# Gate tiles issued by SyncE between the row moves, and a new hand-written order of all steps

## The chip, the core and the metric

The kernel runs on one NeuronCore of a Trainium2 chip. The metric is the device time of one execution in microseconds (us), the median of several runs. Engines are named as in the profile: PE is TensorE (PEld its weight loads), DVE is VectorE, ACT is ScalarE, POOL is GpSimd, and SP is SyncE, which here only issues DMAs.

## What is computed

The reference is one conditional block on x of 32 x 128 tokens by 512 features, read as 8 x 1024 x 512 with 32 conditions of 512 (all in float32):

```python
m = mask[:, :, None]
shift, scale, gate_msa = jnp.split(jax.nn.silu(t) @ ada_w + ada_b, 3, axis=1)
norm = jnp.where(m, _layernorm(x) * (1.0 + scale[:, None]) + shift[:, None], 0.0)
fwd = gelu(norm @ ssm_w1 + ssm_b1) @ ssm_w2 + ssm_b2
bwd = flip(gelu(flip(norm) @ bwd_w1 + bwd_b1) @ bwd_w2 + bwd_b2)
x = x + gate_msa[:, None] * jnp.where(m, fwd + bwd, 0.0)
shift_mlp, scale_mlp, gate_mlp = jnp.split(jax.nn.silu(t) @ ffada_w + ffada_b, 3, axis=1)
ff_norm = _layernorm(x) * (1.0 + scale_mlp[:, None]) + shift_mlp[:, None]
return x + gate_mlp[:, None] * (gelu(ff_norm @ ff_w1 + ff_b1) @ ff_w2 + ff_b2)
```

Masked tokens are few. The first half (the part under the mask) is done for those tokens alone in the opening, some 82 us. The second half, the feed-forward with 512 -> 1024 -> 512 features for all 4096 tokens, is the rest, and only the rest is touched by the change.

## The kernel before, in words

**Tiling.** The 32 batches of 128 tokens are worked in four pairs (p = 0 to 3) of two sides; a side is four batches (G = 4, 512 tokens). Both products of the feed-forward are done by Strassen's scheme in the variant of Winograd, with seven block products instead of eight: the first product has seven streams (1, 2, 5, 6, 3, 7, 4) of seven products each (`6P5` is product P5 of stream 6; L1155), the second product has P1, P5, P2, P6 for two column blocks U and V (`P1U0`; L1387) and three inner products, P3, P7 and P4, that are cut into seven again (`6i3` is part 6 of P3; L1473). What is saved in matmuls is paid in additions on DVE, POOL and ACT.

**What stands around the matmuls.** In the first product, `j` steps (L1207, DVE) add a finished PSUM bank to earlier results and so free the bank; `g` steps (L1125, ACT) apply the gelu. For the second product, `sa0`, `se0`, `sa1`, `se1` (L1283, ACT) seed the PSUM accumulators a_o and e_o with the bias; a_o takes the bank that stream 3 leaves, so `sa0` waits for `3j21`. `k51` and `ke1` (L1303 and L1307, ACT) keep and re-seed the second column block, before `P2V`. `C1i3`, `C5i3` and so on (L1500, ACT) copy inner products out of PSUM. `F00` (L1294, DVE) adds two blocks of the hidden layer.

**The next pair.** While pair p is multiplied, pair p+1 is made ready: `b` steps (L937, DVE) take statistics, POOL forms the root (L945), `n0i` (L955, a DVE TENSOR_SCALAR) and `n1i` (L959, ACT) normalise batch i of side 0 and side 1 into xn, `z` steps (L1808, DVE) transpose 32x32 blocks in place. Then 32 small DMAs `m` (L991, 64 KB each, 16 for a side, issued by SP) move the turned rows from xn to xT, and 32 `c` steps (L968, ACT) scale and shift xT in place. All four `z` of a side come before its first `m`, and all 16 `m` of a side before its first `c`. At the end of the pair, `nW1` and `nW2` (L1109, SP) load weight sums and `n1P1`, `n1P5` and so on are the first products of the next pair.

**The gate.** The output of the feed-forward is multiplied by the gate (L1349 on POOL for side 0, L1331 on DVE for side 1). A gate tile is 128 x 4 x 512 float32, 1 MB, read from gate_rows in DRAM and spread to all partitions (`gate_tile`, L912 to L919). `lg0` and `lg1` load that of side 0 and of side 1. It lies in the same SBUF buffer as weight sums of the first product: gate 0 comes after `7P4` has read its buffer, gate 1 after the last product of stream 4.

**What sets the order.** From about 82 us on all five engines are scheduled by hand: every step is put under its name, and `steps.run(ORDER.get(p, "").split())` issues the steps of pair p in the order of a table of names, one table for each pair. Each engine works off its own instructions in that order, and waits by semaphores for the others. The table also fixes what stands behind what on SP.

Of the kernel before, what the change touches and what calls it, by code (L numbers as in the profile page):

```python
# [22 lines left out]
def kernel(  # L23
# [49 lines left out]
    nc = tc.nc  # L73
# [839 lines left out]
    def gate_tile(p, side):  # L913
        t = gp.tile([P, G, D], F32, tag=f"g{side}", name=f"gate_{p}_{side}", bufs=1)
        nc.gpsimd.dma_start(
            t,
            gate_rows[ts(2 * p + side, G), :].unsqueeze(0).to_broadcast([P, G, D]),
        )
        return t  # L919
# [345 lines left out]
    class SecondProduct:  # L1265
# [9 lines left out]
        def load_gate(self, side):  # L1275
            self.gate[side] = gate_tile(self.p, side)
# [362 lines left out]
    def windows(put, q, f, first, last):  # L1639
# [50 lines left out]
        for w in range(first, last):  # L1690
# [6 lines left out]
            6P5 5P3 6P1 load1 6c5 5k12 6s 3P5 5P7 b00 6P2 x17 6w12 b01 6P6 5j22 6k11 6w22 load0 3P1  # L1697
            6a11 5P4 b02 3c5 6e 5k21 6P3 6P7 3w22 b03 3s b10 6k12 b11 3P6 W3 w30 3P2 7P5 6j22 b12
            7c5 3w12 7P1 6P4 v0 w20 6a12 7s r0 6j21 W4 3k11 4P5 7P2 7w12 3e 6a22 n00 7P6 b13 3P7
            7w22 3P3 4P1 7k11 v1 7e L11 3j22 7P7 n03 n02 4c5 3k12 3P4 r1 4s 7j22 se0 l1 6a21 7P3 4P6  # L1700
            g1222 3j21 sa0 z00 L22 4P2 n01 7P4 7k12 n12 z01 z02 n13 L12 4k11 g2222 z13 4w12 n10 P1U0
            4w22 7j21 F00 P1U1 4e z03 se1 sa1 L21 m003 g2211 4P7 z12 z10 m032 g1221 w70 m013 4j22
            P1V0 P1V1 g2122 w71 m002 w21 4P4 m012 n11 lg0 F02 4P3 g22L P5U0 z11 m001 P5U1 w72 m023
            4j21 F12 m103 m022 T0 g2121 lg1 m133 F10 m100 4k12 w22 m021 m121 k50 m120 w23 m131 ke0
            P5V0 P5V1 m000 m110 k51 ke1 P2U0 m132 g2212 w31 m123 P2U1 m011 m113 m111 m010 B0 P2V1
            m112 P2V0 K000 T1 P6U1 B1 w40 m130 m102 m122 m101 P6U0 c103 w32 c130 w41 c122 U0 c101
            G000 c111 U1 K001 R000 E0 S1i3 c131 w42 m033 m030 c110 5i3 m020 S2i3 1i3 P6V0 c123 m031
            S1i7 C5i3 C1i3 S3i7 5i7 c100 c020 6i3 C5i7 G001 w43 c003 c032 V6i3 S2i7 J30 1i7 P6V1
            S3i3 c012 S4i3 c120 C1i7 c132 w33 c121 w73 c113 6i7 c011 c000 c133 7i3 c002 3i3 c102
            V6i7 E1 C7i3 c010 7i7 2i3 S4i7 c112 V7i3 K010 C7i7 J70 J31 S1i4 R001 3i7 2i7 V7i7 c030  # L1710
            5i4 c001 S2i4 A1 c022 1i4 c013 c031 4i3 J71 C1i4 4i7 E20 c021 6i4 G110 S3i4 A2 n1P5 K011
            G010 C5i4 E21 n1c5 G011 V6i4 n1P1 S4i4 nW1 n1s R010 c033 7i4 J40 c023 2i4 R110 G111 R111
# [9 lines left out]
            3k11 3e 7P6 b11 7w12 6j21 W4 7P2 v0 3P7 6a22 3P3 b12 7k11 4P5 3j22 4P1 3P4 3k12 x27 7e
            4c5 F00 4s 6a21 3j21 7P7 7w22 b13 7j22 se0 sa0 L11 g2211 7P3 4P6 4P2 v1 g1222 7P4 r0 r1
            P1U0 n01 n00 lg0 g1221 4k11 n03 7k12 L12 4w12 F02 l1 n02 P5U0 z01 n12 z00 n13 z03 n11
            z02 n10 L22 m023 4e m012 P5U1 z10 4w22 7j21 z13 z11 sa1 m001 m033 k50 P1U1 m013 L21 4P7
            z12 se1 m032 4P3 m022 m011 g22L P1V0 ke0 4j22 m002 4P4 m000 g2122 m030 P2U0 T0 4j21 m111
            m103 lg1 g2121 F10 m110 g2222 m003 4k12 P1V1 F12 B0 g2212 P5V1 m121 m031 P5V0 m122 T1
            m021 m112 k51 m120 m101 P2U1 B1 ke1 m020 m100 m010 P2V1 K000 m133 P2V0 K001 m131 U0 m113
            c012 P6V1 G000 m130 m132 c022 c020 U1 c002 c003 m102 P6V0 R000 S1i3 c011 c023 E1 5i3
            S2i3 c000 1i3 C5i3 S1i7 S3i3 c001 m123 c111 P6U1 c112 c123 c122 5i7 c120 c133 c110 P6U0  # L1730
            C5i7 c021 C1i3 1i7 c013 6i3 c010 E0 S2i7 V6i3 C1i7 c132 S4i3 n1P1 c102 c130 S3i7 6i7 J30
            c101 c100 c103 G001 S4i7 V6i7 7i3 c113 c121 2i3 3i3 C7i3 c131 c033 V7i3 K010 S1i4 J70
            5i4 S2i4 2i7 J31 C5i4 A1 c030 7i7 1i4 3i7 C7i7 G010 A2 n1P5 V7i7 C1i4 J71 6i4 A3 S3i4
            S4i4 E20 R010 4i3 V6i4 G110 c032 K011 n1c5 4i7 J40 n1s R110 7i4 E21 2i4 c031 3i4 V7i4
            n1P2 n1P6 G111 o00 n2P5 C7i4 n1k11 J41 G100 R100 A4 n1e n2c5 nt11 n2P1 4i4 G011 R011
            n1P3 n1k12 n2s nt12 G101 nt10 R101 nW1 n1P7 R001 n2P2 n1j22 n2P6 o10 n5P5 o01 n2k11 X0
            n5P1 n5c5 n1P4 nt13 nW2 R111 o11 n2w12 n2e nt20 nt22 n2P7 n5s n2w22 nt23 nx30 nt21 nx31
# [12 lines left out]
            4k12 k51 ke1 P2V1 P2V0 m132 m033 P6U1 K000 lg1 c023 m101 c000 m123 P6U0 m112 c010 m131  # L1750
# [367 lines left out]
```

## Time and profile before

| what | us |
|---|---|
| three runs: median (lowest to highest) | 459.79 (458.73 to 461.62) |
| the profiled execution: time | 461.43 |
| its span, first to last instruction | 459.7 |
| PE busy in the span | 440.8 (96%) |
| DVE / POOL / ACT busy | 337.8 / 266.4 / 205.0 |

The span is what the views show, in us from its start; 1.73 us of the profiled execution's time lie outside. Matmuls are pipelined and their ends are modelled, so that neighbouring rows overlap by some 0.15 us: what a matmul group takes is read from the distance of starts. A row of the timeline gives start, duration, engine, line, operation, the tiles written and read, the shapes, the number of instructions, and in brackets the idle time of the engine before it with what ended that.

### The profile page before, as it was taken

The page shows a single profiled execution, that of the slowest core. Times are in us where ns is not written, and L with a number is a line of the kernel's source. Part 1 is how long each engine was busy: PE and PEld are TensorE (multiplying, and loading weights), DVE is VectorE, ACT ScalarE, POOL GpSimd, SP SyncE. Part 2 cuts the span into 40 slices and gives each one's busy share as a digit, 9 for nine tenths or more (in the row PEclk, how much of TensorE's full clock was granted, in tenths as well). Part 3 has the DMA queues.
Part 4 walks back from the last instruction along what each step waited for, and adds up shares of the span by engine and source line. Part 5 has one row for each costly group of instructions (what it writes and reads, how often), then busy time and mean ns, then how long its engine had stood idle before and what let it go on. Part 6 is the DMA issues. An engine that isn't in the chain of part 4 may idle for free.

```text
span 459.7 us, 7036 instructions
## 1 busy us (share of the span) xinstructions
PE 440.8 (96%) x2435; PEld 374.2 (81%) x2435; DVE 337.8 (73%) x592; ACT 205.0 (45%) x453; POOL 266.4 (58%) x234
## 2 busy tenths in 40 slices
PE   8999999999999999999999999979969999999992
PEld 4884674788888998887889988868869988888992
DVE  5798798789996689889742998995516995444265
ACT  3133126353662963536648435257473344471120
POOL 4211550279923993897449858973395426832891
PEclk9999999999999999999999999999979999999998
DMA  7999449993088108741670197309820273112014
GB/s 256 374 395 398 158 89 323 305 336 119 7 220 122 27 17 315 258 121 80 138 141 13 48 312 234 114 3 186 147 34 1 74 269 109 52 70 115 0 47 140
DMA packets 57044, 70.89 MB, mean 154 GB/s; under 512 B 34740, under 2 KB 36108, under 8 KB 55982
## 3 DMA queue, kind: packets, MB, share of 16 engines
q1 hardware_dynamic: 50590, 59.33, 42.3%
q0 software_dynamic: 4160, 10.54, 7.5%
q10 hardware_dynamic: 2256, 0.54, 0.7%
q8 instruction: 21, 0.34, 0.3%
q14 instruction: 17, 0.14, 0.1%
HBM read 56.71 MB, written 13.70 MB: 153 GB/s over the span
## 4 chain that ended last, share of the span: by engine, by line
PE 70%; DMA 6%; POOL 6%; DVE 6%; issue 5%; SPq 3%; ACT 2%; POOLq 0%; ACTq 0%; DVEq 0%
PE a_m L1155 14%; PE e_m L1155 11%; PE e_o L1387 9%; PE a_o L1387 9%; PE one_P L1473 6%; PE po_s L222 6%; SPq L991 3%; PE a_o L1473 3%; DMA xT<-xn 3%; PE e_o L1473 2%; PE five_P L1473 2%; PE ph_s L681 2%; PE ph_s L205 2%; DMA x<-in_x_dram 1%; ACT xT L968 1%
## 5 line engine op out<-in xcount | busy, mean ns | idle before, releaser
L968 ACT ACTIVATE xT<-xT,modT 128x128 f32<-128x128 f32 x112 | 46.1, 485 | 14.0 <-DMA xT<-xn 13.8
L1182 POOL TENSOR_TENSOR ha<-p_m,ha 128x512 f32<-128x512 f32 x20 | 25.8, 1292 | 45.5 <-ACT ha L1197 36.4
L1349 POOL TENSOR_TENSOR t<-t,gate 128x512 f32<-128x512 f32 x16 | 24.4, 1524 | 44.3 <-ACT t L1343 44.3
L1207 DVE TENSOR_TENSOR hb<-a_m,hb 128x512 f32<-128x512 f32 x40 | 27.2, 679 | 13.4 <-PE a_m L1155 13.3
L1125 ACT ACTIVATE hb<-hb,biasT 128x256 f32<-128x256 f32 x64 | 28.4, 500 | 16.2 <-DVE hb L1207 15.9
L1197 ACT COPY ha<-e_m 128x512 f32<-128x512 f32 x32 | 18.6, 584 | 37.2 <-PE e_m L1155 37.2
L904 POOL DMA_INDIRECT x<-x_rows,slot_i x24 | 30.1, 1255 | 7.7 <-issue 6.2
L1505 DVE TENSOR_TENSOR xn_d<-one_P,xn_d 128x256 f32<-128x256 f32 x24 | 10.1, 422 | 30.7 <-PE one_P L1473 24.4
L1387 PE MATMUL a_o<-fw,ha 128*128 128x256 f32 x128 | 29.7, 380 | 3.0 <-ACT a_o L1283 3.0
L1387 PE MATMUL a_o<-t,s 128*128 128x256 f32 x128 | 31.3, 395 | 0.0
L1387 PEld LDWEIGHTS a_o<-fw,ha 128*128 128x128 f32 x128 | 24.2, 190 | 6.7 <-ACT a_o L1283 3.4
L1387 PE MATMUL e_o<-fw,s 128*128 128x256 f32 x128 | 29.1, 379 | 0.0
L1387 PE MATMUL e_o<-fw,ha 128*128 128x256 f32 x128 | 28.6, 379 | 0.0
L222 PE MATMUL po_s<-w,h_s 128*128 128x512 f32 x64 | 28.4, 594 | 0.0
L1182 POOL TENSOR_TENSOR hb<-p_m,hb 128x512 f32<-128x512 f32 x20 | 26.1, 1307 | 2.6 <-DVE hb L1207 2.0
L1387 PEld LDWEIGHTS a_o<-t,s 128*128 128x128 f32 x128 | 24.8, 199 | 3.3
L1387 PEld LDWEIGHTS e_o<-fw,s 128*128 128x128 f32 x128 | 24.3, 190 | 3.3
L1387 PEld LDWEIGHTS e_o<-fw,ha 128*128 128x128 f32 x128 | 24.3, 190 | 3.3
L1125 ACT ACTIVATE ha<-e_m,biasT 128x256 f32<-128x256 f32 x48 | 19.9, 467 | 13.7 <-PE e_m L1155 12.6
L1155 PE MATMUL a_m<-xT,tw 128*128 128x256 f32 x96 | 24.8, 382 | 0.3 <-DVE e_m L1188 0.3
L1169 ACT COPY p_m<-e_m 128x512 f32<-128x512 f32 x27 | 15.8, 585 | 18.9 <-PE e_m L1155 18.8
L1155 PE MATMUL e_m<-s,fw 128*128 128x256 f32 x92 | 23.7, 380 | 0.0
(281 smaller groups left out, 1160.5 us busy)
## 6 DMA issues: line engine op xcount, KB each, us to landing
x<-in_x_dram SPq DMA_DIRECT2D x16, 512.0 KB, 6.4
tw<-t_rows SPq DMA_DIRECT2D x16, 512.0 KB, 4.2
gate<-gate_rows POOLq DMA_DIRECT2D x8, 1024.0 KB, 6.5
out_dram<-x SPq DMA_DIRECT2D x15, 512.0 KB, 4.0
xT<-xn SPq DMA_DIRECT2D x104, 64.0 KB, 2.2
tw<-t_rows SPq DMA_DIRECT2D x16, 384.0 KB
ada_f<-in_L_cond_ffada_w_dram SPq DMA_DIRECT2D x4, 768.0 KB, 14.7
ada_a<-in_L_cond_ada_w_dram SPq DMA_DIRECT2D x4, 512.0 KB, 3.5
```

The lines of the kernel that those rows point to most:

```text
L222: nc.tensor.matmul(po, h[f][:, ts(i, P)], w[:, f, :], start=(f == 0 and seeded is None), stop=(f == HC - 1), skip_group_check=seeded is no ...
L904: nc.gpsimd.indirect_dma_start(out=xs[i // G][i % G // 2][:, i % 2], out_offset=None, in_=x1_rows, in_offset=bass.IndirectOffsetOnAxis(ap= ...
L968: nc.scalar.activation(out, src, AF.Identity, bias=shift, scale=scale)
L1125: nc.scalar.activation(dst[:, n], src[:, n], AF.Gelu_apprx_tanh, bias=biasT[:, f : f + 1])
L1155: nc.tensor.matmul(bank[:, ts(n, QT)].rearrange("p (i b c) -> p i b c", i=2, c=R), self.w_block(j, product)[:, ts(n, P)], self.x_block(j, ...
L1169: nc.scalar.copy(self.p5[j], self.fives[j].rearrange("p (n s) -> p n s", n=2))
L1182: nc.gpsimd.tensor_tensor(self.place(RESULT[j], c), self.p5[j], other, ALU.add)
L1197: nc.scalar.copy(self.place(RESULT[j], c), src)
L1207: nc.vector.tensor_tensor(dst, a, other, ALU.add)
L1349: nc.gpsimd.tensor_tensor(view, view, self.gate[side][:, 2 * c : 2 * c + 2, part], ALU.mult)
L1387: nc.tensor.matmul(bank[:, ts(i, D // 2)], src[:, k, ts(i, P)], w[:, k, :], start=False, stop=True, skip_group_check=True,)
L1473: nc.tensor.matmul(out[:, i % out.shape[1]], src[:, k, ts(i, P)], w[:, k, :], start=(start and (i == 0 or out.shape[1] == 1) and k == 0), ...
```

## The change

Two things are changed. `gate_tile` issues its DMA from SP's queue instead of POOL's:

```diff
     def gate_tile(p, side):
         t = gp.tile([P, G, D], F32, tag=f"g{side}", name=f"gate_{p}_{side}", bufs=1)
-        nc.gpsimd.dma_start(
+        nc.sync.dma_start(
             t,
             gate_rows[ts(2 * p + side, G), :].unsqueeze(0).to_broadcast([P, G, D]),
         )
```

And the tables of all four pairs hold the same names in another order. The number of steps, and of instructions on every engine but SP and POOL, stays the same. One row of each table, pair 2:

```diff
-            6P4 b10 n02 W4 3P6 6j21 7P2 z02 7k11 3e 6a22 7w12 n00 x36 7P6 7e 4P5 4P1 3P7 4c5 7w22
+            r0 6P4 7P2 3e b10 7P6 3w22 6j21 7k11 n00 W4 7e 6a22 4P5 n03 z03 4P1 3P7 L11 4c5 7w22
...
```

What that does to the engines is shown at three places, all in pair 2. In the names, a number behind a tile's name is a buffer's; xT_0 and xn_0 are side 0, xT_1 and xn_1 side 1 of the next pair.

First SP, from the last weight sums of pair 2's first product to the first of the next pair's. Before:

```order
L1109 DMA tw_1_2279<-t_rows 128x768
L991 DMA xT_0_2518<-xn_0_2432 32x8x64 x14
L991 DMA xT_1_2614<-xn_1_2552 32x8x64
L991 DMA xT_0_2518<-xn_0_2432 32x8x64
L991 DMA xT_1_2614<-xn_1_2552 32x8x64 x3
...
L991 DMA xT_1_2614<-xn_1_2552 32x8x64 x12
L1109 DMA tw_0_2899<-t_rows 128x1024
```

Now:

```order
L1109 DMA tw_1_2297<-t_rows 128x768
L991 DMA xT_0_2520<-xn_0_2442 32x8x64 x9
L915 DMA gate_0_2586<-gate_rows 128x2048
L991 DMA xT_0_2520<-xn_0_2442 32x8x64 x7
L991 DMA xT_1_2614<-xn_1_2565 32x8x64 x16
L915 DMA gate_1_2842<-gate_rows 128x2048
L1109 DMA tw_0_2895<-t_rows 128x1024
```

The gate of side 0 stands behind nine moves, that of side 1 behind all 32, and all moves of side 0 come before the first of side 1. In pair 0 the first gate stands ahead of all moves, in pair 1 behind seven; the second stands behind all 32 in both. In pair 3, which has no moves, both stand behind each other, side 1 first, as they did on POOL.

Then DVE in pair 2, where the last batches of side 0 are normalised while stream 3 ends (a_m_3, its bank, is freed by the second L1207 on it). Before:

```order
L1175 TENSOR_TENSOR e_m_4_2453<-a_m_4_2454,ha_2221 128x512
L955 TENSOR_SCALAR xn_0_2432<-x_2270,mv_0_2344,rstd_0_2345 128x4x4x32
L1207 TENSOR_TENSOR hb_2222<-a_m_3_2365,hb_2222 128x2x256
L1808 STREAM_TRANSPOSE xn_0_2432<-xn_0_2432 128x4x4x32
L1207 TENSOR_TENSOR hb_2222<-a_m_7_2402,hb_2222 128x2x256
L955 TENSOR_SCALAR xn_0_2432<-x_2268,mv_0_2344,rstd_0_2345 128x4x4x32
...
L937 BN_STATS st_1_2_2489<-x_2328 128x6
```

Here the row left out is the second L1207 on a_m_3 (`3j21`), right behind the fourth L955. Now:

```order
L1808 STREAM_TRANSPOSE xn_0_2442<-xn_0_2442 128x4x4x32 x2
L1207 TENSOR_TENSOR hb_2230<-a_m_3_2357,hb_2230 128x2x256
L1175 TENSOR_TENSOR e_m_4_2448<-a_m_4_2449,ha_2229 128x512
L1207 TENSOR_TENSOR hb_2230<-a_m_7_2411,hb_2230 128x2x256
L955 TENSOR_SCALAR xn_0_2442<-x_2289,mv_0_2344,rstd_0_2345 128x4x4x32
L1808 STREAM_TRANSPOSE xn_0_2442<-xn_0_2442 128x4x4x32
...
L937 BN_STATS st_1_1_2490<-x_2322 128x6
L938 BN_AGGR mv_1_2347<-st_1_1_2490 128x2
L955 TENSOR_SCALAR xn_0_2442<-x_2291,mv_0_2344,rstd_0_2345 128x4x4x32
```

Again `3j21` is the row left out; it now stands behind three of the four L955, and the fourth follows it.

Last ACT in pair 2, where the scaling of xT meets the copies of the second product. Before:

```order
L1343 COPY t_100_2674<-e_o_1_2554 128x512
L968 ACTIVATE xT_0_2518<-xT_0_2518,modT 128x4x32 x5
L968 ACTIVATE xT_1_2614<-xT_1_2614,modT 128x4x32
L968 ACTIVATE xT_0_2518<-xT_0_2518,modT 128x4x32
L968 ACTIVATE xT_1_2614<-xT_1_2614,modT 128x4x32 x2
L968 ACTIVATE xT_0_2518<-xT_0_2518,modT 128x4x32 x2
L1500 COPY xn_d_2705<-one_P_2697 128x2x128
...
L1500 COPY xn_d_2705<-five_P_2692 128x2x128
```

Now:

```order
L1307 COPY e_o_0_2484<-a_o_0_2485 128x512
L968 ACTIVATE xT_0_2520<-xT_0_2520,modT 128x4x32 x2
L1303 COPY p_o_1_2632<-e_o_1_2532 128x512
L1307 COPY e_o_1_2532<-a_o_1_2533 128x512
L968 ACTIVATE xT_0_2520<-xT_0_2520,modT 128x4x32 x4
L1343 COPY t_000_2647<-e_o_0_2484 128x512
...
L1343 COPY t_100_2668<-e_o_1_2532 128x512
L968 ACTIVATE xT_0_2520<-xT_0_2520,modT 128x4x32
L1500 COPY xn_d_2703<-one_P_2690 128x2x128
L968 ACTIVATE xT_1_2614<-xT_1_2614,modT 128x4x32
...
L1500 COPY xn_d_2703<-five_P_2680 128x2x128
```

The first copy of an inner product (L1500 from one_P, `C1i3`) stood behind three scalings of side 1; now it stands ahead of them all, and the second (from five_P, `C5i3`) behind two. On the other hand two scalings of side 0 now stand ahead of `k51` and `ke1` (L1303 and L1307 on e_o_1).

More of the change, by code (lines that the diff above doesn't have):

```diff
@@ L1696 @@
         0: """
[L1697 to L1712, printed above, removed]
@@ new lines @@
+            sa1 m002 w70 z10 P5U1 m033 4P4 g2122 g22L m021 w22 4j21 P1V1 m012 z11 4P3 m022 g2121 k50
+            F12 P1V0 F10 m020 P5V1 w31 m011 m133 m030 B0 P5V0 w32 ke0 k51 w23 P2U1 P2U0 m023 T1 4k12
+            m010 m032 ke1 K000 T0 P2V0 m111 m102 B1 m100 m031 P2V1 P6V1 w40 m113 K001 w71 m112 G000
+            U0 m000 m130 m101 U1 m110 w72 R000 m001 m003 S1i3 P6V0 w41 c030 m132 S2i3 c033 5i3 c001
+            C5i3 m120 c032 1i3 c022 m122 m121 C1i3 w42 m131 P6U1 c003 6i3 c013 S1i7 m103 c023 V6i3
@@ L1722 @@
[L1722 to L1737, printed above, removed]
@@ new lines @@
+            7k12 g2211 z02 b13 g1221 4P2 F02 v1 n00 L12 z00 m033 r1 l1 g2212 4w12 m031 4k11 m013 L22
+            m032 7P4 n10 P1U1 P1U0 P5U1 7j21 n12 sa1 P5U0 n11 4e n13 se1 z12 m012 m000 m020 lg0 k50
+            g2222 4P7 L21 4P3 P1V0 m030 z13 4w22 m001 4j22 g2122 z10 ke0 4P4 T0 m010 m003 m002 4j21
+            P1V1 m011 z11 m103 P2U1 g2121 F10 m023 g22L m130 m022 m132 F12 m131 m100 m021 T1 m101 B0
+            m122 P5V0 P5V1 4k12 k51 P2U0 ke1 K000 B1 P2V0 U0 c000 G000 m102 P2V1 R000 U1 c012 m111
@@ L1770 @@
[L1770 to L1774 removed]
+            6P1 6P5 5P3 5P7 5j22 6c5 3P1 3P5 5P4 6s W3 6P2 5k12 6P6 5k21 6k11 6w12 6e 7P5 6a11 3c5
```

100 lines of the change are left out of this document (61 added, 39 removed).

## The prediction

> **What bounds the kernel now.** I read the busy shares first, then PE stretch by stretch, then what ended PE's idle times, then the rows around them.
>
> ```profile
> PE 440.8 (96%) x2435; PEld 374.2 (81%) x2435; DVE 337.8 (73%) x592; ACT 205.0 (45%) x453; POOL 266.4 (58%) x234
> ```
>
> PE is the bound on average. The windows show how evenly; they are pairs 0 to 3 and what follows the last matmul (length, then PE's busy time and records, ending with the granted clock and DMA).
>
> ```profile
> 98.20:188.46 90.26, 89.58 (x494) 79.93 (x493) 78.03 (x123) 48.09 (x108) 62.87 (x48) 1.00 0.50 139
> 188.46:278.94 90.48, 89.49 (x494) 80.05 (x493) 70.13 (x113) 48.61 (x108) 65.70 (x51) 1.00 0.48 135
> 278.94:377.77 98.83, 92.27 (x493) 82.20 (x492) 72.16 (x108) 48.71 (x110) 58.94 (x49) 0.97 0.44 110
> 377.77:451.11 73.34, 73.34 (x421) 66.63 (x419) 36.15 (x54) 26.19 (x58) 46.33 (x38) 1.00 0.20 69
> ```
>
> Pairs 0, 1 and 2 hold the same matmuls, and pair 2 takes 8.4 us more. How far each lies over its matmuls alone follows from undisturbed rows of the chain of waits:
>
> ```profile
> 103.96 2.59 PE a_m L1155 x12
> 415.06 10.36 PE e_o L1387 x48
> 349.00 0.89 PE one_P L1473 x8
> ```
>
> A product of the first kind (x4) takes 0.863, a unit of the second (x8) 1.727, an inner part (x8) 0.89. A pair has 49, 16 and 21 of them: 42.3 + 27.6 + 18.7 = 88.7 us. So pair 0 loses 1.6, pair 1 1.8, pair 2 10.1. PE's waits from 98 us on name most of it:
>
> ```profile
> PE one_P L1473 <- ACT xn_d L1500: 3.6, 1, 3.6
> PE a_o L1387 <- ACT a_o L1283: 3.0, 1, 3.0
> PE a_m L1155 <- DVE e_m L1175: 1.0, 1, 1.0
> ```
>
> The two long ones are in pair 2:
>
> ```profile
> 306.61 3.72 PE L1387 MATMUL a_o<-fw,ha 128*128 128x256 f32 x16 [3.00 <-ACT a_o L1283]
> 340.70 2.05 PE L1473 MATMUL one_P<-inner_more,si_P 128*128 128x128 f32 x8 [3.56 <-ACT xn_d L1500]
> 342.54 3.62 PE L1387 MATMUL a_o<-t,s 128*128 128x256 f32 x8
> 345.96 1.25 PE L1473 MATMUL one_P<-inner_more,ha 128*128 128x128 f32 x8
> 347.05 1.06 PE L1473 MATMUL five_P<-t,si_P 128*128 128x128 f32 x8
> ```
>
> Behind the second wait PE runs at half speed: from start to start the three groups take 1.84, 3.42 and 1.09 us where 0.89, 1.73 and 0.89 are usual, 2.84 us lost (the 0.97 above is this). So pair 2 lost 3.0 + 3.56 + 2.84 = 9.4 by these two waits, and 0.7 otherwise.
>
> **The first wait, the seed.** DVE, ACT and POOL around 303 us:
>
> ```profile
> 300.90 4.43 DVE L955 TENSOR_SCALAR xn<-x,mv,rstd 128x512 f32<-128x512 f32 x1
> 305.25 0.68 DVE L1207 TENSOR_TENSOR hb<-a_m,hb 128x512 f32<-128x512 f32 x1
> ```
>
> ```profile
> 305.96 0.59 ACT L1283 COPY a_o<-fb 128x512 f32<-128x512 f32 x1 [4.15 <-DVE hb L1207]
> ```
>
> ```profile
> 302.56 1.26 POOL L1220 TENSOR_TENSOR hb<-hb 128x512 f32<-128x512 f32 x1
> 303.79 1.25 POOL L1220 TENSOR_TENSOR ha<-ha 128x512 f32<-128x512 f32 x1
> 305.12 1.34 POOL L1182 TENSOR_TENSOR ha<-p_m,ha 128x512 f32<-128x512 f32 x1
> ```
>
> ```profile
> L955 DVE TENSOR_SCALAR xn<-x,mv,rstd x12: 507/586/4431, 113.8 to 300.9; 128x512 f32<-128x512 f32 x12
> ```
>
> ```profile
> 98.20:188.46 90.26, 3.17 (x4) 1.00 0.50 139
> 188.46:278.94 90.48, 2.00 (x4) 1.00 0.48 135
> 278.94:377.77 98.83, 7.60 (x4) 0.97 0.44 110
> ```
>
> One normalisation takes 4.43 us where the median is 0.59 (the last three rows are the busy time of the four L955 of each pair). It ends at 305.33, just behind the first gap in POOL's row of additions (305.04 to 305.12). `3j21`, behind it on DVE, is late by 3.8, and so is the seed.
>
> **The second wait, the moves.** The 32 moves on SP in pairs 0, 1 and 2; then for pair 2 SP's waits for its own DMAs, and the landing times (min/median/max) of moves and of gates:
>
> ```profile
> 127.38 23.64 SPq L991 DMA_DIRECT2D xT<-xn  x32
> ```
>
> ```profile
> 218.79 22.72 SPq L991 DMA_DIRECT2D xT<-xn  x32
> ```
>
> ```profile
> 309.04 27.01 SPq L991 DMA_DIRECT2D xT<-xn  x32
> ```
>
> ```profile
> SPq L991 <- DMA xT<-xn: 5.1, 4, 2.9
> ```
>
> ```profile
> DMA to landing us min/median/max: 2.2/2.3/9.9
> ```
>
> ```profile
> DMA to landing us min/median/max: 8.0/9.0/10.1
> ```
>
> In pair 2 the moves take 27.0, of which SP waits 5.1 for moves that land late, while two gates of 1 MB are under way beside them. Without these waits a move takes 21.9 / 32 = 0.68 to issue, and lands 2.2 later. The first move is itself late, since its transposes stand behind the slow L955 on DVE. At the end of this the copy sits behind scalings of side 1 on ACT:
>
> ```profile
> 337.89 2.42 ACT L968 ACTIVATE xT<-xT,modT 128x128 f32<-128x128 f32 x6 [3.18 <-DMA xT<-xn]
> 340.21 0.35 ACT L1500 COPY xn_d<-one_P 128x256 f32<-128x256 f32 x1
> ```
>
> **The change part by part.** *Gates off POOL.* Eight issues of 0.6 us leave POOL, and its wait in front of one:
>
> ```profile
> 318.40 0.55 POOL L915 DMA_DIRECT2D gate<-gate_rows  x1 [4.53 <-PE a_m L1155]
> 327.44 1.69 POOL L1349 TENSOR_TENSOR t<-t,gate 128x512 f32<-128x512 f32 x1 [8.48 <-ACT t L1343]
> ```
>
> The next POOL step idles 8.5 us for ACT anyway: worth 0. If that cover were gone it would be worth at most 0.6 a gate.
>
> *Gates onto SP.* Each costs SP about one issue, 0.7. That delays the moves behind `lg0` and, behind `lg1`, only `nW1`. What a gate does to moves behind it in one queue the trace does not show. The bounds: nothing, since even alone on POOL's queue it lands in 4.9 (pair 3's first, below) and SP could issue seven moves in that time; and the 5.1 us of pair 2, where two gates disturb. I take 1.5, nearer the lower end, since one gate is left in the way and the other waits until all moves are issued. The gates' users are far enough: gate 1 now leaves behind the last move, at about 330 in pair 2, lands by 340 even at the worst 10.1 us, and is first read by DVE at 358.3 (the first row; the second is all pairs together). In pair 0 it leaves some 24 us behind the first move, at 152, and has landed by 162, against 167.4.
>
> ```profile
> L1331 DVE TENSOR_TENSOR e_o<-e_o,gate x2: 693/696/699, 358.3 to 368.2; 128x512 f32<-128x512 f32 x2
> ```
>
> ```profile
> L1331 DVE TENSOR_TENSOR e_o<-e_o,gate x8: 683/692/700, 167.4 to 449.2; 128x512 f32<-128x512 f32 x8
> ```
>
> ```profile
> DMA to landing us min/median/max: 4.9/6.0/7.1
> ```
>
> By the Trainium skill, page "DMA: Bandwidth & Descriptors", section "Issuing engines are not separate DMA queues", all issuers share the same 16 engines, so another queue alone changes only who spends the issue time; the late landings above, with the gates on another queue, agree. By that rule alone the sum would be 0, which is the first rival; it says nothing against `lg1` leaving after the moves.
>
> *The seed.* In pair 2 `3j21` now has three L955 ahead of it instead of four, one statistic less and one transpose more: 0.6 + 0.85 - 0.62, some 0.8 us of plain work less. Its product 3P4 still stands three products ahead of P1 on PE. The seed is due at 303.4 (306.6 less the wait and the overlap of the rows), 3P4 is done 2.6 before, at 300.8, and `3j21` and the copy take 0.6 each: 1.4 us to spare. Whether an L955 meets a closed row of POOL again is the unknown: at best 0, at worst the same 3.8. In the rows above pairs 0 and 1 have at most 1.2 us of it among eight, and in pair 2 the other three L955 have 3.17 together, so one of twelve went beyond what is to spare. I take none: the 3.0 us goes. Bounds: 0 to -3.0.
>
> The Trainium skill, page "SBUF — State Buffer", section "Who interferes with whom", says that such an operation and a POOL one hold a shared port in turn, each for its whole instruction. The trace agrees, except that here DVE was passed over for three POOL instructions and not one. By the rule as it stands an L955 waits for one addition at most, 1.25, and the seed would be safe.
>
> *The copy.* The last transpose of side 0 (`z02`) stands some 3.5 us of DVE work behind `3j21`, done at 301.5, so the first move leaves near 305.0 instead of 309.0 if no L955 waits. With 21.9 + 0.7 + 1.5 the last move is issued by 329.1 and has landed by 331.3. `C1i3` no longer waits for side 1. `C5i3` does, behind two scalings of it and one of side 0, 0.4 each (2.42 / 6 above): it ends at 332.9. Counting PE's products on from 303.4 without waits (16 units of the second kind, 3 products of the first, 3 inner parts: 32.9), part 7 of P3, which needs it, starts at 336.3. So 3 us to spare, and both 3.56 and the 2.84 of slow clock go. If nothing of this came true (first move at 309.5, 5.1 of waits), the copy would end at 341, 2 us late or more again, depending on the seed. Bounds: 0 to -6.4.
>
> *Side 0's scalings ahead of `k51`.* Added risk: the first 16 moves must have landed by the time at which PE needs `ke1` for `P2V`, less the 2.0 of two scalings and two copies: `P2V` comes 10 units and 3 products behind 303.4, at 323.3, so at 321.3. 305.0 + 16 x 0.68 + 0.7 + 1.5 + 2.2 = 320.3: hidden, but by 1.0 us only; this is the tightest place that I find. What it costs without that cover is the last rival below.
>
> *Everything else in the order.* Pair 1's wait of 1.0 comes from an L1294 that is also held up; it now stands elsewhere. Other steps have less distance than before, others more. Pairs 0 and 1 lose 1.7 each to such things, and I take that for pair 2 too, with bounds for the whole of -1.7 (one pair loses nothing) to +4 (one more wait as long as the longest, with little of the clock). Near the middle, and because of the 1.0 us just named, I take +1.0.
>
> **The sum.** Pair 2 goes from 98.8 to 88.7 + 1.7 = 90.4: -8.4; the rest +1.0. Against the profiled execution 461.4 - 8.4 + 1.0 = **454.0 us**. The median of the runs, 459.8, lies 1.6 below that execution; since I take the waits to be what varies, the end without them is the same, and the median falls by 5.8 (1.3%).
>
> **Rivals.** *Hidden anyway:* the same bytes share the same engines, and what pair 2 gains another place loses: about 459.8. For it speaks that pair 2's waits come of chance meetings, which any order has; against it, that three of four pairs have next to none. *Half of it:* an L955 is held up again ahead of `3j21` (the 3.0 stays: 457.0) or the moves stay slow (3.56 + 2.84 stay: 460.4). For it speaks that POOL's row of additions is as long as before. *Slower, the gate in front of the moves:* SP sends moves into the queue behind 1 MB, and they land like the slowest above, 9.9 instead of 2.2. With a first move at 309.5, 16 moves, the gate and 5.1 of waits, side 0 has landed at 328.4, 7.1 us late for `ke1`; whether the seed's 3.0 is part of that or not, PE loses 7.1 + 2.84 of clock and the usual 1.7, 11.6, 1.5 more than now. In pair 0 side 0's last move is the 25th: 127.4 + 25 x 0.68 + 0.7 + 5.1 + 2.2 = 152.4, and `C1i3` ends five scalings and two copies later, at 155.1, 1.7 after PE's part 6 of P3 is due (153.4, by the same count of products); with the clock 4.5. Together 461.4 + 6.0 = 467.4. It decides once side 0 lands over 1.0 us later than I reckon, and costs all of this from some 7 us on. Against it speaks pair 0, which ran with both gates among its moves and lost 0.2 us to ACT:
>
> ```profile
> PE five_P L1473 <- ACT xn_d L1500: 0.2, 1, 0.2
> ```
>
> **How the numbers follow.** Forecast 0.50 (449.5 to 456.5; the lower end is 88.7 in pair 2, 1.7 less elsewhere and no new wait); half 0.25; hidden 0.13; slower 0.12. A change of over 1%, 4.6 us, is about what a measurement tells from none: below 455.2 faster, above 464.4 slower. Of the forecast's half a little lies above 455.2, and of the half gains hardly any below: faster 0.46, same 0.42, slower 0.12. The range that holds it 8 times in 10 takes in half gains and no change: 449.5 to 462.
>
> **What would show it.** Right: pair 2 near 90 us like pairs 0 and 1; no PE wait on L1283 or L1500 over 1 us; no clock below 1.00 in the pairs; 32 moves in 23 us or less in pair 2; gate 1 issued right behind the last move. Wrong: an L955 or L1294 of over 3 us with PE waiting behind it; PE waiting in e_o of `P2V` or in an inner part behind L968; SP waiting over 3 us for its own DMAs behind `lg0`.

## The result, and the profile after

The changed kernel takes 453.29 us (median of 4 runs, 452.98 to 454.02); the kernel before took 459.26 us beside it. The ratio of the runs is 0.9865, 95% interval 0.9824 to 0.9907: 6.0 us or 1.3% faster. The forecast was 454.0. The profiled execution took 454.02 us with a span of 452.3.

The windows of pairs 0 to 3 (length, then busy time and records of PE, PEld, DVE, ACT and POOL, the granted clock, the share of DMA and GB/s):

```profile
99.11:188.60 89.49, 89.09 (x494) 80.27 (x492) 78.35 (x125) 48.50 (x108) 63.58 (x46) 1.00 0.47 130
188.60:281.18 92.58, 89.21 (x494) 80.10 (x492) 70.76 (x111) 47.95 (x107) 64.08 (x50) 1.00 0.50 140
281.18:370.24 89.06, 88.95 (x493) 80.24 (x492) 69.06 (x107) 48.66 (x110) 57.99 (x46) 1.00 0.44 123
370.24:443.60 73.36, 73.33 (x421) 66.63 (x419) 37.37 (x55) 26.31 (x58) 45.73 (x36) 1.00 0.18 63
```

Pair 2 went from 98.8 to 89.1, 0.4 over its matmuls alone, and its clock is back at 1.00. Pair 1 takes 2.1 more than before, pair 0 0.8 less, and the first product of pair 0 starts 0.9 later. PE's waits, all from 85 us on:

```profile
PE e_m L1155 <- DVE e_m L1188: 1.9, 1, 1.9
PE one_P L1473 <- POOL hb L1462: 1.5, 1, 1.5
PE one_P L1473 <- DVE xn_d L1505: 0.4, 1, 0.4
```

Neither L1283 (the seed) nor L1500 (the copy) is there any more; both long waits are in pair 1 now. The seed in pair 2, on DVE, ACT, PE, and DVE again:

```profile
303.12 0.65 DVE L1207 TENSOR_TENSOR hb<-a_m,hb 128x512 f32<-128x512 f32 x1
```

```profile
303.81 0.59 ACT L1283 COPY a_o<-fb 128x512 f32<-128x512 f32 x1 [2.18 <-DVE hb L1207]
```

```profile
305.35 1.89 PE L1387 MATMUL a_o<-fw,ha 128*128 128x256 f32 x8
```

```profile
304.50 1.78 DVE L955 TENSOR_SCALAR xn<-x,mv,rstd 128x512 f32<-128x512 f32 x1
```

The seed ends at 304.40, 0.95 before PE can use it. A normalisation was held up again (1.78 us), but it is the fourth, which now stands behind `3j21`: only the first move pays for it. SP in pair 2, and ACT and PE where side 0 is scaled ahead of `ke1` (L1307):

```profile
308.38 5.82 SPq L991 DMA_DIRECT2D xT<-xn  x9
314.30 0.54 SPq L915 DMA_DIRECT2D gate<-gate_rows  x1
314.89 17.95 SPq L991 DMA_DIRECT2D xT<-xn  x23
332.88 0.60 SPq L915 DMA_DIRECT2D gate<-gate_rows  x1
```

```profile
322.62 0.88 ACT L968 ACTIVATE xT<-xT,modT 128x128 f32<-128x128 f32 x2 [2.66 <-DMA xT<-xn]
...
324.00 0.57 ACT L1307 COPY e_o<-a_o 128x512 f32<-128x512 f32 x1
...
334.47 0.37 ACT L1500 COPY xn_d<-one_P 128x256 f32<-128x256 f32 x1 [4.20 <-PE one_P L1473]
```

```profile
322.13 7.07 PE L1387 MATMUL e_o<-fw,ha 128*128 128x256 f32 x32
```

The first move leaves 27.2 us behind the pair's start (30.1 before; the forecast's 305.0 is 26.1). The scalings wait for the last move of side 0, and `ke1` ends at 324.57. `P2V` is the second half of the PE row and starts at 322.13 + 2 x 1.73 = 325.58: 1.0 us to spare at the place called tightest. The copy at 334.47 waits for PE and no longer for a move.

### The profile page after: what moved, and what is told of

The parts are those of the page before. It is cut to its first block, busy times and chain, and to the rows that moved or that the text cites. A ratio compares the mean times of both kernels' runs of the same rounds, so it can differ in the third digit from the quotient of the medians.

```text
span 452.3 us, 7030 instructions
## 1 busy us (share of the span) xinstructions
PE 436.5 (97%) x2435; PEld 372.1 (82%) x2435; DVE 336.8 (74%) x592; ACT 204.8 (45%) x453; POOL 263.9 (58%) x226
## 4 chain that ended last, share of the span: by engine, by line
PE 72%; DMA 11%; DVE 6%; POOL 5%; issue 5%; ACT 0%; POOLq 0%; SPq 0%; DVEq 0%; ACTq 0%
PE a_m L1155 17%; PE e_m L1155 13%; PE e_o L1387 12%; PE a_o L1387 11%; PE one_P L1473 6%; DMA fw<-in_L_cond_ff_w_dram 3%; PE po_s L222 3%; DMA w<-in_L_cond_bwd_w_dram 3%; PE a_o L1473 3%; PE five_P L1473 2%; PE e_o L1473 2%; DMA x_wide<-t_s 2%; POOL x L904 2%; POOL t L1349 1%; DMA x<-in_x_dram 1%
## 5 line engine op out<-in xcount | busy, mean ns | idle before, releaser
L1182 POOL TENSOR_TENSOR ha<-p_m,ha 128x512 f32<-128x512 f32 x20 | 25.5, 1274 | 48.2 <-ACT ha L1197 36.8
L904 POOL DMA_INDIRECT x<-x_rows,slot_i x24 | 31.5, 1311 | 8.2 <-issue 6.6
L1207 DVE TENSOR_TENSOR hb<-a_m,hb 128x512 f32<-128x512 f32 x40 | 27.2, 679 | 10.0 <-PE a_m L1155 7.3
L1387 PE MATMUL a_o<-t,s 128*128 128x256 f32 x128 | 29.6, 379 | 0.0
L1387 PEld LDWEIGHTS a_o<-fw,ha 128*128 128x128 f32 x128 | 24.3, 190 | 3.3
L1387 PEld LDWEIGHTS e_o<-fw,ha 128*128 128x128 f32 x128 | 24.3, 190 | 3.3
L1387 PEld LDWEIGHTS a_o<-t,s 128*128 128x128 f32 x128 | 23.7, 190 | 2.9
L1398 DVE TENSOR_TENSOR e_o<-a_o,p_o 128x512 f32<-128x512 f32 x16 | 11.1, 693 | 18.1 <-PE a_o L1387 17.1
L1155 PE MATMUL a_m<-xT,tw 128*128 128x256 f32 x96 | 24.3, 379 | 0.0
L1155 PE MATMUL e_m<-s,fw 128*128 128x256 f32 x92 | 23.7, 381 | 0.0
```

The source lines that it names most:

```text
L904: nc.gpsimd.indirect_dma_start(out=xs[i // G][i % G // 2][:, i % 2], out_offset=None, in_=x1_rows, in_offset=bass.IndirectOffsetOnAxis(ap= ...
L1155: nc.tensor.matmul(bank[:, ts(n, QT)].rearrange("p (i b c) -> p i b c", i=2, c=R), self.w_block(j, product)[:, ts(n, P)], self.x_block(j, ...
L1182: nc.gpsimd.tensor_tensor(self.place(RESULT[j], c), self.p5[j], other, ALU.add)
L1207: nc.vector.tensor_tensor(dst, a, other, ALU.add)
L1387: nc.tensor.matmul(bank[:, ts(i, D // 2)], src[:, k, ts(i, P)], w[:, k, :], start=False, stop=True, skip_group_check=True,)
```

## The experiments

Twelve kernels, timed in three groups, each beside runs of the kernel before (medians 459.05, 458.26 and 458.82). The ratio is worked out from the runs themselves, not from the two medians. The theory to test is the prediction's: the order of pair 2 removes two waits, and the queue is worth about nothing; its rival is that the queue does it. A third, on POOL's row, was formed after the first group.

| kernel | median us | ratio to before (95%) |
|---|---|---|
| order_alone | 457.68 | 0.9968 (0.9942 to 0.9995) |
| queue_alone | 459.83 | 1.0003 (0.9964 to 1.0042) |
| seed_alone | 459.00 | 0.9996 (0.9968 to 1.0024) |
| copy_alone | 458.01 | 0.9973 (0.9948 to 0.9998) |
| gates_on_act | 455.28 | 0.9936 (0.9898 to 0.9975) |
| pool_issues_kept | 457.15 | 0.9957 (0.9933 to 0.9982) |
| both_by_hand | 456.32 | 0.9954 (0.9929 to 0.9980) |
| pair2_alone | 454.70 | 0.9909 (0.9878 to 0.9940) |
| changed_again | 453.06 | 0.9891 (0.9864 to 0.9918) |
| pair1_back | 452.87 | 0.9885 (0.9857 to 0.9913) |
| gates_front | 455.98 | 0.9937 (0.9913 to 0.9962) |
| gather_moved | 459.74 | 1.0025 (0.9999 to 1.0050) |

**order_alone.** The changed kernel with

```diff
-        nc.sync.dma_start(
+        nc.gpsimd.dma_start(
```

and `lg0` and `lg1` moved in the tables to where POOL is at those times.

> The new order, with the gates issued by POOL again, each put into POOL's row at the time at which SP issued it in the changed kernel. Theory 'order' (the two waits of pair 2 went because of where the steps stand, the queue is worth about nothing): 453 to 455 us, pair 2 within 1 us of the 89.1 that it takes in the changed kernel, SP waiting under 3 us for its own DMAs in pair 2. Rival 'queue' (the moves land early because the gates no longer come through POOL): the moves land late again, pair 2 at 94 us or more, 458 to 460 us. With the gates on POOL the 0.7 us per gate on SP is saved, so a gain of up to 0.5 us on the changed kernel is possible under 'order'.

Pair 2 took 90.8 us, 1.7 more than in the changed kernel, where "order" allowed 1.0 and "queue" asked for 94 or more. But the time is 457.7, as "queue" says. The reason of "queue" does not fit: the moves of pair 2 took 23.9 us, no longer than in the changed kernel; side 0 was ready 15.3 us behind the first move (14.2 there), and PE did not wait for it. What changed is DVE, shown here at two places (pair 0, pair 2), each with the rows of POOL where its hold-up ends (a step is held up when it stands far longer than it takes alone):

```profile
154.88 3.60 DVE L1829 TENSOR_TENSOR fw<-t,fw 128x256 f32<-128x256 f32 x1
```

```profile
156.94 1.25 POOL L1349 TENSOR_TENSOR t<-t,gate 128x512 f32<-128x512 f32 x1
158.27 1.26 POOL L1356 TENSOR_TENSOR x<-t,x 128x512 f32<-128x512 f32 x1
```

```profile
342.67 3.92 DVE L1091 TENSOR_TENSOR sx<-xT 128x512 f32<-128x512 f32 x1
```

```profile
344.78 1.26 POOL L1462 TENSOR_TENSOR hb<-hb 128x512 f32<-128x512 f32 x1
346.12 1.60 POOL L1462 TENSOR_TENSOR hb<-hb,si_P 128x512 f32<-128x512 f32 x1
```

The first takes 0.75 in the changed kernel, the second 1.66. Each of the long ones ends just behind the first gap in POOL's row (158.19 to 158.27, 346.04 to 346.12). PE waits behind them: in pair 0 0.7 for DVE's L1420, which stands behind the L1829, in pair 2 0.9 for DVE's L1021, behind the L1091. By pairs the profiled execution is 1.6, 0.7 and 1.7 us longer than the first one of the changed kernel. The new theory: each gate on POOL puts 0.6 us into that row, which shifts all additions behind it against DVE's steps.

**queue_alone.** The kernel before with

```diff
-        nc.gpsimd.dma_start(
+        nc.sync.dma_start(
```

> The old order, with the gates issued by SP at the places of their old names. Theory 'order': no gain, 459 to 462 us, pair 2 still over 96 us with a wait of about 3 us for the seed (L1283) and one of 3 us or more for the copy (L1500). In pair 2 the second gate now stands ahead of 15 of the moves in their own queue, so the copy may come later still. Rival 'queue': 454 to 456 us, and moves that take 24 us or less in pair 2.

No change, as "order" said, but not for its reason. The longest of PE's waits in pair 2, and SP there (between the two rows stand 8 more moves and, ahead of and behind them, the gates):

```profile
PE a_o L1387 <- ACT a_o L1283: 3.0, 1, 3.0
...
```

```profile
310.17 7.79 SPq L991 DMA_DIRECT2D xT<-xn  x12
...
325.49 9.83 SPq L991 DMA_DIRECT2D xT<-xn  x12
```

The seed's wait is as before, and here the clock fell behind it, to 0.50 for 2 us. The copy's is gone in pair 2, though two gates now stand ahead of moves in their own queue: the 32 moves take 25.2 us with 1.2 of gates in it, where they took 27.0 with the gates on POOL's queue. In pair 0 it is the other way round: 24.9 us with two gates in it, and 23.6 before. What pair 2 gained (96.0 us), pair 0 partly lost (91.8, with 1.6 of wait for its copy).

**seed_alone.** Pair 2's table of the kernel before:

```diff
-7k12 n01 3j21 b12
+7k12 3j21 n01 b12
```

> The old order and POOL's queue; in pair 2 one name is moved, the normalisation n01 now stands behind 3j21 instead of ahead of it. The seed should no longer wait: the 3.0 us on L1283 goes. Theory 'one delay' (both waits of pair 2 hang on the same late normalisation, and the moves start behind n01 and z01 as before): PE starts the second product 3 us earlier and waits as much longer for the copy, 6 to 7 us instead of 3.6, so 459 to 461 us, no change. Rival 'two delays' (the two waits are independent terms that add up, as the prediction's sum has them): the wait for the copy stays 3.6 us, 456 to 457 us.

No change in the median. PE's waits in pair 2:

```profile
PE one_P L1473 <- ACT xn_d L1500: 3.9, 1, 3.9
PE e_o L1387 <- DVE s L1294: 1.1, 1, 1.1
```

The seed's wait is gone, a third of it came back as a wait for L1294 (behind `n01` on DVE), and the copy's wait grew by 0.4 only (3.95 and 3.56), not by 3. In the profiled executions pair 2 is 2.8 us shorter than before (96.05); the median does not show it. So "one delay" has the time right and most of the mechanism wrong: `n01` was shorter here (3.3 us), and the moves took 26.1.

**copy_alone.** Also pair 2's table of before:

```diff
-S1i3 m100 c112 S3i3 c002 E0 c102 5i3 1i3 c120 c003 c011 C1i3 c033 P6V0 C5i3 S2i3
+S1i3 m100 S3i3 c002 E0 5i3 1i3 c003 c011 C1i3 c033 P6V0 C5i3 c112 c102 c120 S2i3
```

> The old order and POOL's queue; in pair 2 three names are moved, the scalings c112, c102 and c120 (two of side 1) now stand behind C5i3, so that the first copies of inner products wait for moves of side 0 alone. Theory 'queue behind side 1': the wait of 3.6 us and the half clock behind it (2.8 us) go, the seed's 3.0 us stays: 452.5 to 454 us. Rival 'late moves' (the copies still stand behind scalings of side 0 whose moves land late too): 2 us or more of the wait stay, with the clock: 456 to 459 us.

The median fell by 1.0, not by 6. In the profiled execution pair 2 takes 94.0 and has no wait for the copy; but the clock's loss did not go with it: 1.4 us of it now follow the seed's wait.

```profile
309.66 5.11 PE L1387 MATMUL a_o<-fw,ha 128*128 128x256 f32 x16 [3.01 <-ACT a_o L1283]
```

These 16 matmuls took 3.72 in the kernel before, behind the same wait. That explains 1.4 us of what is missing. In the profiled execution another 2.2 were lost in pair 0, whose instructions are those of before (92.5 us with 1.0 of wait for its copy, against 90.3 and 0.2): pair 0 changes from execution to execution. And the profiled execution of before was a long one (461.4 against a median of 459.1).

**both_by_hand.** The edits of the last two together.

> The old order and POOL's queue with the edits of seed_alone and copy_alone together: four names moved in pair 2. Theory 'in series' (each of the two waits only hides or shifts the other, both must go): pair 2 takes 90 to 92 us, no wait of PE on L1283 or L1500 over 1 us in it, 453 to 455.5 us. Rival 'medians add' (the profiled execution overstates both waits; the typical execution gains what the two alone gained, 0.0 and 1.0): 457 to 459 us.

Between the two ranges: 456.3, with 94.0 us in pair 2, more than "in series" said. Both waits are gone, and the copy's has moved one product on, to `C1i7`, which now finds 14 scalings ahead of it; ACT, then PE behind it:

```profile
336.41 5.49 ACT L968 ACTIVATE xT<-xT,modT 128x128 f32<-128x128 f32 x14 [1.78 <-DMA xT<-xn]
341.81 0.35 ACT L1500 COPY xn_d<-one_P 128x256 f32<-128x256 f32 x1
```

```profile
342.67 1.86 PE L1473 MATMUL one_P<-t,hb 128*128 128x128 f32 x8 [2.67 <-DVE xn_d L1505]
```

**pair2_alone.** The gates on SP, and only pair 2's table from the changed kernel.

> The gates on SP, the old order in pairs 0, 1 and 3 and the new one in pair 2 alone. Theory 'pair 2' (the gain lies in pair 2's table): pair 2 takes 89 to 91 us, and against queue_alone (459.8), which differs in that table only, the time falls by 5 to 7: 453 to 455 us. Rival 'as a whole' (the tables only fit each other, and pair 2 meets other hold-ups behind another pair 1): pair 2 at 92 us or more, 456 to 459 us.

As "pair 2" said: 454.7 us, pair 2 89.85. Against queue_alone, timed in another group, that is 5.1 less; against the kernel before beside it 3.6, where the whole change gains 5.8 to 6.0. In the profiled execution, a long one (457.4), PE waits 2.2 us for a copy in pair 0, which has the old order with two gates among its moves and takes 93.95.

**pool_issues_kept.** The changed kernel and

```diff
+    def dummy(p, k):
+        nc.gpsimd.dma_start(
+            scr[:, 2 * p + k : 2 * p + k + 1, :],
+            gate_rows[0:1, 0:4].unsqueeze(0).to_broadcast([P, 1, 4]),
+        )
```

called where order_alone has its gates.

> The changed kernel with its gates on SP, and in addition eight small DMAs (128 pieces of 16 bytes into a tile that nobody reads) issued by POOL at the places where order_alone issues its gates; this is extra work that the reference does not have. Theory 'row': most of the loss of order_alone comes back without any megabyte on POOL's queue, 456.5 to 458.5 us, with an L1829 of about 3.6 us near 155 us and an L1091 of over 3 us near 342 us. Rival 'queue': 453 to 454.5 us like the changed kernel.

As "row" said, to the step: 457.15 us, and DVE (lines are 8 higher in this kernel, L1837 is L1829, L1099 is L1091) is held up at the same two:

```profile
154.95 3.61 DVE L1837 TENSOR_TENSOR fw<-t,fw 128x256 f32<-128x256 f32 x1
...
343.92 3.48 DVE L1099 TENSOR_TENSOR sx<-xT 128x512 f32<-128x512 f32 x1
```

So the 4 us of order_alone come from eight issues on POOL, not from the megabytes. Whether it is the 0.6 us of time alone that does it, or something else in such an issue, no run separates. Nor is all of the loss traced: pair 1 of this execution lost 2.3 us as well, most of it by a clock of 0.52 to 0.63 in the 4 us behind a wait that the changed kernel has too (1.99 us for L1196, its L1188).

**gates_on_act.** The changed kernel with `nc.scalar.dma_start` for the gates.

> The new order, with the gates issued by ACT at about the times at which SP issued them in the changed kernel, so that they come through a queue of their own again, as in order_alone, but leave POOL's row of additions alone. Theory 'row' (order_alone lost its 4 us because eight issues of 0.6 us shift POOL's additions against DVE's steps, which then stand for 3.6 and 3.9 us): 453 to 455 us, no L1829, L1091 or L955 on DVE over 2.7 us. Rival 'queue' (what counts is that gates and moves share a queue): 457 to 458 us like order_alone.

455.3 us, and no held-up step of DVE over 2.2: nearer to "row", but 2 us short. The profiled execution shows two places. In pair 2, with one gate among the moves as in the changed kernel, side 0 is ready 16.0 us behind the first move instead of 14.2, and PE waits 0.7 for `ke1`. In pair 1, with both gates issued among them, the 32 moves take 26.67 us on SP (23.1 in the changed kernel, where one gate stands among them), and PE waits 1.9 for a copy, with a clock of 0.54 to 0.61 in the 4 us behind it. How much of the second is due to the queue and how much to the second gate is not shown.

```profile
217.74 26.67 SPq L991 DMA_DIRECT2D xT<-xn  x32
```

**changed_again.** The changed kernel once more.

> The changed kernel as it is, on the chip of the three runs beside it. If what holds DVE up is set by the order and not by chance, the same steps take the same times as in its first profile: L955 1.2 us in pair 1 and 1.8 in pair 2, L1829 1.5 at most, L1021 2.5; PE waits 1.9 and 1.5 us at the same two places of pair 1, pair 2 takes 89 to 90 us, and the median is 453 to 454.5 us. If they were chance meetings, they stand elsewhere, and the time spreads as that of before does (over 5 us).

Mostly not chance: the L955 of pair 2 takes 1.78 again, that of pair 1 1.16, L1829 1.52, pair 2 89.06 again, median 453.06. What differs is pair 1 (90.9 and 92.6): the wait for L1462 is not there this time. There a hold-up changed sides. The L1021 of pair 1 took 2.54 in the first profile and takes 1.30 now, and POOL's addition beside it, 1.30 then, takes 2.25; whether the wait hangs on this is not shown. The first row is of the first profile, the second of this one:

```profile
253.36 2.54 DVE L1021 TENSOR_TENSOR s<-xT 128x1024 f32<-128x1024 f32 x1
```

```profile
252.57 1.30 DVE L1021 TENSOR_TENSOR s<-xT 128x1024 f32<-128x1024 f32 x1
```

L955 and the windows of pairs 1 and 2, now:

```profile
L955 DVE TENSOR_SCALAR xn<-x,mv,rstd x12: 532/806/1782, 113.9 to 302.0; 128x512 f32<-128x512 f32 x12
```

```profile
187.81:278.69 90.88, 88.97 (x494) 80.19 (x493) 68.96 (x111) 47.81 (x107) 63.81 (x50) 1.00 0.51 143
278.69:367.75 89.06, 88.95 (x494) 80.23 (x492) 68.93 (x107) 48.61 (x110) 57.72 (x46) 1.00 0.44 122
```

**pair1_back.** The old table in pair 1, else the changed kernel.

> The changed kernel with the old table in pair 1 alone (gates on SP in all pairs). In the changed kernel pair 1 takes 92.6 us, with two waits of 1.9 and 1.5 us that the old table does not have (90.5). Theory 'tables add': 451 to 452.5 us. Rival 'as a whole' (behind another pair 1 the additions of pair 2 meet DVE elsewhere, or the old pair 1 has waits of its own behind the new pair 0): 453 to 456 us.

452.87 us, between the two ranges and the same as changed_again. Behind the new pair 0 the old pair 1 has 92.5 us and waits of its own (0.8 twice for L1188, 1.1 for L1175), as "as a whole" has it; pair 2 did not suffer (89.65). The experiments show no version that is measurably faster than the changed kernel.

**gates_front.** Pair 2's table of the changed kernel:

```diff
-k50 lg0 4k12
+k50 lg0 lg1 4k12
```

(`lg1` leaves its old place.)

> The changed kernel; in pair 2 the second gate stands right behind the first, so that 2 MB lie in SP's queue ahead of seven moves of side 0 and all of side 1. Rival of the prediction 'gate in front of the moves': the moves behind it land 5 us or more late, PE waits for the scalings of side 0 ahead of P2V, or for the copies, 3 us or more in all with half clock behind it, 457 to 461 us. Theory 'issue time' (a gate costs SP 0.6 us and little else): the moves land within 4 us of being issued, 453 to 454.5 us.

456.0 us, 2.9 more than changed_again. ACT and PE at the tight place:

```profile
326.51 0.88 ACT L968 ACTIVATE xT<-xT,modT 128x128 f32<-128x128 f32 x2 [5.78 <-DMA xT<-xn]
...
327.89 0.57 ACT L1307 COPY e_o<-a_o 128x512 f32<-128x512 f32 x1
```

```profile
328.60 3.69 PE L1387 MATMUL e_o<-fw,ha 128*128 128x256 f32 x16 [2.07 <-ACT e_o L1307]
```

From the first move (309.17) to the scalings it is 17.3 us, 3.1 more than the 14.2 above; with 1.0 to spare PE should wait 2.1, and it waits 2.07. So the rival's place and its point of decision hold, and its price does not: a second megabyte in front of the moves costs 3.1 of landing.

**gather_moved.** Pair 2's table of before:

```diff
-b11 x37 4s 7P7 3P3 n03 6a21 3j22
+b11 4s 7P7 3P3 n03 6a21 x37 3j22
```

> The kernel before, with one name moved in pair 2: the gather x37 on POOL now stands between two additions (behind 6a21) instead of ahead of them, so that POOL's row has a hole where the normalisation of 4.4 us stood for it. Theory 'closed row' (DVE's normalisation stands until POOL's additions leave a gap): it takes 0.6 to 1.5 us, the seed's wait of 3.0 us is gone, the first move of pair 2 leaves 3 to 4 us earlier against the pair's start, and the copy's wait shrinks below 1.5 us; 454 to 456.5 us. Rival 'other cause' (traffic, or the data): L955 takes 4.4 us again, 458 to 459.5 us.

No gain: the hole came too early. POOL, then DVE:

```profile
298.05 1.27 POOL L1216 TENSOR_TENSOR hb<-hb 128x512 f32<-128x512 f32 x1
299.48 1.04 POOL L904 DMA_INDIRECT x<-x_rows,slot_i  x1 [0.16 <-issue]
...
303.01 1.25 POOL L1220 TENSOR_TENSOR ha<-ha 128x512 f32<-128x512 f32 x1
304.34 1.34 POOL L1182 TENSOR_TENSOR ha<-p_m,ha 128x512 f32<-128x512 f32 x1
```

```profile
297.77 1.84 DVE L955 TENSOR_SCALAR xn<-x,mv,rstd 128x512 f32<-128x512 f32 x1
...
301.33 3.22 DVE L955 TENSOR_SCALAR xn<-x,mv,rstd 128x512 f32<-128x512 f32 x1
```

The third L955, 0.62 in the kernel before, stands until the hole (POOL's addition ends at 299.32, it ends at 299.61); the fourth begins behind the hole and stands until the next gap (304.26, it ends at 304.55). The expectation's time was wrong; both hold-ups end where its mechanism has them, but one became two. In the profiled execution (458.3, below the median) both long waits of pair 2 are shorter for it, 1.8 for the seed and 2.2 for the copy, and pair 2 takes 95.7; the median shows no gain.

## Why the prediction was right, and where not

*What bounds the kernel.* Right: pair 2 was the place. But its 10.1 us of loss were those of one long execution: the runs of before spread from 456.8 to 464.0 us, and the profiled one, 461.4, lies 2.4 above the median of 35. (The three terms of the matmuls alone add up to 88.6, not 88.7; nothing hangs on it.) The text allowed for part of that by taking the median's gain as 5.8; it was 6.0.

*The seed.* The 3.0 went, with 0.95 to spare where 1.4 was reckoned. "At best 0, at worst the same 3.8" was answered by 1.8, on the one L955 that had been put behind `3j21`. The estimate "one of twelve" was the wrong way to see it: this hold-up repeats from one profiled execution to the next, to some 0.02 us (4.43, 4.43 and 4.44 in before, queue_alone and copy_alone; 1.78 in both profiles of the changed kernel). Not every hold-up does: the L1021 under changed_again did not.

*The copy.* Right: the 3.6 and the clock's 2.8 went. The first move left 1.1 later than reckoned, which is that L955.

*The gates onto SP.* Taken as 1.5 for a gate among the moves: measured 14.2 us from the first move to the scalings, where 15 issues of 0.65 (5.82 / 9), the gate's own 0.6 and 2.2 of landing make 12.5, so 1.7. The upper bound came from gates on another queue, and that case is not the same. With the new table of pair 2 and one gate among the moves, side 0 is ready 14.2 us behind the first move when the gate is in the moves' own queue, 15.3 when it comes from POOL (order_alone) and 16.0 from ACT (gates_on_act). So the first rival's reading, that another queue only changes who spends the issue time, fails there. For the whole row of 32 moves the runs do not agree: with two gates under way it takes 25.2 us in pair 2 of queue_alone against 25.6 to 27.0 with POOL's queue (before and the four kernels with its queue and order), but in pair 0 24.9 and 25.5 (queue_alone, pair2_alone; 23.7 and 24.3 without the 1.2 of the gates' issues) against 23.6 to 24.4.

*Side 0's scalings ahead of `k51`.* Right to the tenth, 1.0 to spare, but by luck: the first move left 1.1 later than reckoned, and side 0 was ready 14.2 behind it instead of 15.3. gates_front and gates_on_act show what lies behind this place: 3.1 and 1.8 us later PE waits 2.1 and 0.7.

*"Gates off POOL: worth 0".* This step failed. It was priced by the one wait that stands behind a gate on POOL. In the new order eight issues on POOL cost some 4 us (order_alone 457.7, pool_issues_kept 457.15, against 453.1). The bound it named, 0.6 a gate, makes 4.8 for eight, but for another reason, POOL's own cover. What the two kernels share is a row of additions in which the same two steps of DVE are held up; that the 0.6 us shifted this row is argued from them, and in both kernels pair 1 lost time that is not traced to it. In the old order taking the issues away brought nothing (queue_alone). By medians the order alone brings 1.4, the queue alone nothing that can be measured (its ratio is 1.0003), both together 6.0: most of the gain belongs to neither part.

*The rivals.* "Hidden anyway" and "half of it" did not come: neither long wait is left in pair 2 in either profile. "Slower" has its place confirmed and its price not: it took 5.1 of waits behind one gate, which cost 1.7, and two gates ahead of the moves made 2.1 us of waiting, 2.9 in the median, where 6.0 was reckoned for the whole.

*The rest, +1.0.* In the first profile it was +2.3 (pair 0 -0.8, pair 1 +2.1, the opening +0.9, the end +0.1), in the second -0.3, and pair 2 was 1.3 better than reckoned. So against the first profiled execution the total is right to the tenth only because two errors of 1.3 us cancel; against the medians it is 0.7 and 0.9 high.

*What stays open.* Why order_alone lost 0.7 in pair 1, and what copy_alone's median lost beyond the clock and pair 0, was not settled. The order's own gain with the gates on POOL depends on where in POOL's row they are put; only one such place was tried.

## What to carry to other kernels

Price an instruction that leaves an engine by what it does to the rhythm of the row that it leaves, not only by the wait behind it: here 0.6 us on an engine with 42% idle time moved the end by half a us each. Two parts of a change that are worth 1.4 us and nothing alone can be worth 6 us together, so measure them crossed. And before giving a wait a price, look for the next step behind it that hangs on the same late transfers.

## What the runs showed of the hardware

A DVE step that reads two SBUF operands, or an L955, can stand through several of POOL's additions. Where it gets in, it ends a set time behind the end of one of them: of the five cases shown (one in the prediction, two in order_alone, two in gather_moved) four end 0.29 us behind it, the L1829 of 256 elements and the L955 of 512, and the L1091 of 512 ends 0.55 behind. In these five that addition is the first with a gap of 0.08 us or more behind it, and the longest step stood from within one addition through the three after it. But a gap is not needed. In the kernel before an L1829 of 256 elements that began at 152.49, inside the first row below, ended at 153.87, 0.28 behind the end of that row, and POOL's next row follows without a gap:

```profile
152.25 1.34 POOL L1462 TENSOR_TENSOR hb<-hb 128x512 f32<-128x512 f32 x1
153.55 1.45 POOL L1349 TENSOR_TENSOR t<-t,gate 128x512 f32<-128x512 f32 x1
```

What decides whether DVE gets in between two rows without a gap is open.

The Trainium skill, page "SBUF — State Buffer", section "Who interferes with whom", says that these two engines share a port, that steps of these kinds can contend for it, and that whoever issues first has it for its whole instruction. The runs agree on the kinds. They add that the turn does not always go to DVE after one addition: in the longest case it went to POOL three times more.

PE's clock falls behind some waits of about 2 us and more and not behind others of the same length. The shortest wait with a lower clock behind it is the one of 1.85 us in gates_on_act; behind the 3.00 of the kernel before the clock stayed at 1.00. The same wait of 1.92 us in pair 1 stands in gates_front and in changed_again:

```profile
197.56 1.44 PE L1155 MATMUL e_m<-xn_sy,tw 128*128 128x256 f32 x4 [1.92 <-DVE e_m L1188]
198.79 1.91 PE L1155 MATMUL a_m<-xn_sy,tw 128*128 128x256 f32 x4
```

```profile
197.66 1.13 PE L1155 MATMUL e_m<-xn_sy,tw 128*128 128x256 f32 x4 [1.92 <-DVE e_m L1188]
198.63 1.03 PE L1155 MATMUL a_m<-xn_sy,tw 128*128 128x256 f32 x4
```

In the first the granted clock from 197.5 to 201.0 was 0.61, and 1.7 us more were lost behind the wait than in the second, where it stayed at 1.00. So a wait's price has a part that changes from execution to execution. Whether the changed kernel spreads less because its longest wait is 1.9 us is not shown: its ten runs lie within 3.6 us and those of the kernel before within 7.2, but there are 85 of these beside the twelve kernels.
